# Layer 2's residual loads: issued with the transposes, or two images ahead behind the sums

## The chip, the cores and the metric

The kernel runs on one core of a Trainium2 chip. The metric is the time of one execution on the device in microseconds (us); the kernel before takes 3451.94 us, the median of 3 runs (3447.39 to 3453.05). The engines are named as the profile names them: PE multiplies matrices, DVE and ACT and POOL compute on vectors, SP only issues transfers (DMA).

## The reference

The input is 8 images of 384 channels and 32 x 32 pixels, in float32. Four layers follow one another; each adds its result to its input, and each normalizes its input over groups of 12 channels first:

```python
x = x + L0(_gn(x))   # depthwise 3x3, GELU, attention over the 1024 pixels, projection, batch norm
x = x + L1(_gn(x))   # 4 experts of 384 hidden units, top 2 by a gate
x = x + L2(_gn(x), w, b)   # depthwise 7x7
x = x + L3(_gn(x))   # 1x1, 3x3 and 5x5 branches, mixed by weights from their means, projection

def L2(x, w, b):
    xp = pad(x, 3, mode="reflect")
    return depthwise_conv(xp, w) + b[None, :, None, None]
```

The change is in the layer called 2 here (counted from 0): the depthwise 7x7 convolution, its bias, and the addition of its input, which is called the residual.

## The kernel before

**Tiles.** The 384 channels are three channel tiles `ct` of 128, which is the number of partitions. When layer 1 has finished an image, it writes the image to memory outside the core (`r2mem[ct]`, lines 998 to 1003), where it waits as the residual, and puts the normalized image transposed into `xts[ct]`, for tile 2 by way of `x2mem`.

**The convolution** (lines 1281 to 1324). For each tile there are 8 chunks `c`. A chunk is 7 rows of taps times 16 products of 32 x 32 matrices over all 8 images, thus 112 matmuls; a float32 matmul stands as two records in the trace, so 224 records. Two chunks fill one of the two PSUM tiles, which ACT copies out into `o` (`evict`, line 1236). Each chunk has a set of weights of 532 KB. `next_weights` (line 1035) issues the load of the set three chunks ahead on SP, line 1046, and adds the reflected edges to it on POOL, line 1052. There are three weight buffers (`lw`, line 1027), so a set can be loaded when PE is through with the set three before it.

**Finishing an image.** When tile `ct` has been convolved, `finish_all(ct, o)` (line 1181) finishes its 8 images while PE convolves the next tile. For each image, `finish` (line 1152) is a generator of two steps:

- step one takes an `r2` tile and loads the residual into it (line 1154, 512 KB, on SP), and turns the image back by a transpose on DVE (line 1157);
- step two is the sum of the convolved image, the bias and the residual on DVE (line 1159), the store of the sum to `y2mem` (line 1162, 512 KB, on SP), and statistics: `bn_stats`, and for tiles 0 and 1 sums of the rows and columns at the edge (lines 1170 and 1174 on DVE, 1176 on POOL).

For tiles 0 and 1 `lead` is 8: all first steps come before the first sum. For tile 2 `lead` is 2: the first step of image b + 2 comes ahead of the sum of image b. The pool `ty` (line 1083) has two `r2` buffers, so the load for image b + 2 can start only when the sum of image b has read its buffer. Between the sums of tile 0, `prepare` (line 1138) loads tile 2's images from `x2mem` (line 1143, tile `xn2`) and DVE transposes them (line 985). Late in tile 2's convolution, `prepare3` (line 1202) loads the finished sums again, as halves of images (line 1214), for the convolutions of layer 3.

**What sets the order.** From line 1279 on, PE, ACT, DVE and POOL run their instructions in the order in which the program writes them:

```python
with tc.manual_schedule(engines=ORDERED | {mybir.EngineType.Pool}):
```

SP is not among them. Its instructions are put in order by the framework's scheduler, when it expects each to be ready. The order is fixed when the program is built. SP then works through it one by one: an instruction that waits, for a buffer or for data, holds up all behind it. So the weight loads, the residual loads, the stores and the loads of `x2mem` all stand in one line.

## Time and profile before

| | |
|---|---|
| median of 3 runs | 3451.94 us (3447.39 to 3453.05) |
| the profiled execution | 3453.2 us, of which the span that the profile shows is 3451.5 us |
| busy in the span | PE 3085.5 us (89%), DVE 1610.4 (47%), ACT 1202.3 (35%), POOL 140.8 (4%) |
| the 7x7 convolution with tile 0, nothing to finish (2882 to 2962 us) | PE busy 58.2 of 80.0 us, granted clock 0.89 |
| mostly tile 1, tile 0's images finished (2962 to 3047 us) | PE busy 46.4 of 85.0 us, granted clock 0.84 |
| mostly tile 2, tile 1's images finished (3047 to 3098 us) | PE busy 32.7 of 51.0 us, granted clock 0.80 |
| after it, 3x3 and 5x5 begin, tile 2's images finished (3098 to 3192 us) | PE busy 51.0 of 94.0 us, granted clock 0.57 |

Times within the execution are counted from the start of the span. A line of the timeline gives the start, the busy time, the engine (SPq is SP's queue of issues), the line of the program, the operation, what is written and read, the shape and the number of instructions; in brackets stand the idle time before it and what ended that. The granted clock is the share of full speed that PE got. The wait of a DMA instruction on SP is not busy time; it is seen in the view of waits.

### The profile page before, as it was taken

What the parts mean: (1) busy time and instruction counts of PE and PEld (TensorE: products, weight loads), DVE (VectorE), ACT (ScalarE), POOL (GpSimd) and SP (SyncE); (2) the same over time, 40 slices, a digit from 0 to 9 for tenths busy, and PEclk for the clock granted to TensorE, in tenths of its full rate; (3) what the DMA queues carried; (4) which work ended last, traced back from release to release, by engine and by line L of the source; (5) the groups of instructions that cost most, each with busy time, mean ns of one, the idle gap of its engine ahead of it and who ended that gap; (6) DMA issues with size and microseconds to landing.
All of it is one profiled execution on the core that took longest, in us unless ns stands there. A gap on an engine that the chain in (4) does not pass through costs nothing. (4 is left out here: it accounts for less than half of the span.)

```text
span 3451.5 us, 56137 instructions
## 1 busy us (share of the span) xinstructions
PE 3085.5 (89%) x24960; PEld 1403.8 (41%) x24960; DVE 1610.4 (47%) x2193; ACT 1202.3 (35%) x1147; POOL 140.8 (4%) x320
## 2 busy tenths in 40 slices
PE   3666999999999999999979999999999997555889
PEld 2443334343434343433333444444444444334434
DVE  6778344444454544444442654333333321546164
ACT  3654453535454444445324302122222211123320
POOL 1000000000000000000000000000000000110200
PEclk9998999999999999999989999999999998885989
DMA  6766202011111010110017222022111103556655
GB/s 223 250 235 229 99 21 76 21 60 36 57 39 57 30 61 27 55 42 19 23 49 270 85 90 86 28 67 76 32 63 64 41 8 117 194 171 199 224 198 200
DMA packets 97251, 338.49 MB, mean 98 GB/s; under 512 B 13985, under 2 KB 16777, under 8 KB 92457
## 3 DMA queue, kind: packets, MB, share of 16 engines
q1 hardware_dynamic: 81816, 285.81, 23.9%
q0 software_dynamic: 9184, 32.49, 2.7%
q10 hardware_dynamic: 6000, 16.53, 1.6%
q8 instruction: 197, 3.23, 0.4%
q14 instruction: 54, 0.43, 0.0%
HBM read 236.39 MB, written 101.53 MB: 98 GB/s over the span
## 5 line engine op out<-in xcount | busy, mean ns | idle before, releaser
L548 ACT ACTIVATE e<-sc 128x1024 f32<-128x1024 f32 x512 | 484.2, 1029 | 583.0 <-PE sc L541 582.6
L759 PE MATMUL ph<-xn,w 128*128 128x512 f32 x1152 | 525.0, 594 | 1.2 <-ACT xn L200 1.2
L972 PE MATMUL y<-hs,w 128*128 128x512 f32 x1152 | 519.9, 593 | 1.5 <-DVE hs L957 1.5
L541 PE MATMUL sc<-qT,kT 64*128 64x512 f32 x2048 | 481.7, 607 | 22.1 <-DVE qT L467 15.4
L560 PE MATMUL av<-e,vT 128*64 128x512 f32 x2048 | 468.9, 600 | 0.0
L763 ACT ACTIVATE hs<-ph,b 128x512 f32<-128x512 f32 x192 | 131.7, 686 | 630.9 <-PE ph L759 629.3
L972 PEld LDWEIGHTS y<-hs,w 128*128 128x128 f32 x1152 | 217.8, 190 | 274.4 <-issue 263.5
L759 PEld LDWEIGHTS ph<-xn,w 128*128 128x128 f32 x1152 | 216.3, 190 | 268.3 <-issue 258.8
L541 PEld LDWEIGHTS sc<-qT,kT 64*128 64x128 f32 x2048 | 186.5, 186 | 309.9 <-issue 232.0
L957 DVE TENSOR_TENSOR hs<-hs,cb 128x512 f32<-128x512 f32 x192 | 130.7, 690 | 355.6 <-ACT hs L763 348.6
L560 PEld LDWEIGHTS av<-e,vT 128*64 128x64 f32 x2048 | 135.9, 137 | 318.6 <-issue 318.6
L449 PE MATMUL sc<-y,pw 128*128 128x512 f32 x576 | 254.1, 602 | 12.0 <-DVE kT L467 7.3
L325 PE MATMUL ps<-xt,w 32*32 32x256 f32 x6912 | 161.9, 418 | 106.8 <-issue 106.8
L576 DVE RECIPROCAL inv<-sm 128x512 f32<-128x512 f32 x64 | 214.6, 3353 | 2.2
L1291 PE MATMUL ps<-xt,w 32*32 32x256 f32 x5376 | 135.2, 438 | 82.4 <-POOL w L1052 39.6
L574 DVE LOAD_MASK_SELECT sm<-av x64 | 0.9, 14 | 417.1 <-PE av L560 417.1
L962 DVE SCALAR_TENSOR_TENSOR r<-cb,b,r 128x512 f32<-128x512 f32 x192 | 134.9, 744 | 91.0 <-DMA cb<-cfmem 89.4
L325 PEld LDWEIGHTS ps<-xt,w 32*32 32x32 f32 x6912 | 109.8, 107 | 158.5 <-issue 136.3
L449 PEld LDWEIGHTS sc<-y,pw 128*128 128x128 f32 x576 | 110.4, 193 | 155.2 <-issue 147.2
L350 ACT COPY o<-ps 128x2048 f32<-128x2048 f32 x36 | 134.6, 3739 | 102.0 <-PE ps L325 101.3
L1291 PEld LDWEIGHTS ps<-xt,w 32*32 32x32 f32 x5376 | 91.9, 110 | 124.5 <-issue 56.9
L1236 ACT COPY o<-ps 128x2048 f32<-128x2048 f32 x20 | 73.9, 3694 | 173.2 <-PE ps L1291 151.6
(285 smaller groups left out, 2680.8 us busy)
## 6 DMA issues: line engine op xcount, KB each, us to landing
raw<-y SPq DMA_DIRECT2D x72, 512.0 KB
y<-raw SPq DMA_DIRECT2D x24, 1536.0 KB
xr<-in_x SPq DMA_DIRECT2D x42, 512.0 KB
cb<-cfmem SPq DMA_DIRECT2D x64, 256.0 KB
w<-in_w ACTq DMA_DIRECT2D x36, 384.0 KB
w<-in_w SPq DMA_DIRECT2D x24, 532.0 KB
x<-in_x SPq DMA_DIRECT2D x16, 768.0 KB
z<-z POOLq DMA_DIRECT2D x16, 768.0 KB, 4.3
```

Source lines behind the costliest of these rows:

```text
L325: nc.tensor.matmul(ps[32 * j : 32 * j + 32, i, cc], lhsT=w[r, cc, j, k, :], rhs=xt0s[ct][r, 8 * j + 2 * u + cc, :, k : k + H], start=k == ...
L350: nc.scalar.copy(o.rearrange("p b h (i c) -> p i c (b h)", i=4)[:, :, 2 * u : 2 * u + 2], ps.rearrange("p i c b h -> p i c (b h)"),)
L449: nc.tensor.matmul(ps[:, h, :], lhsT=w[:, ct, pair, :], rhs=y[:, ct, h * HF : (h + 1) * HF], start=ct == 0, stop=ct == NC - 1,)
L541: nc.tensor.matmul(sc[:, s, :], lhsT=kTs[b][r, pair, m * P : (m + 1) * P], rhs=qTs[b][r, pair, h * HF : (h + 1) * HF], start=True, stop=True,)
L548: nc.scalar.activation(e, sc, AF.Exp, scale=1.0 if shifted else HD**-0.5)
L560: nc.tensor.matmul(av[64 * s : 64 * s + 64, :], lhsT=vT[:, m, c0 : c0 + 64], rhs=e[:, s, :], start=m == 0, stop=m == N // P - 1,)
L576: nc.vector.reciprocal(inv, sm)
L759: nc.tensor.matmul(ph, lhsT=w1[:, e, ct, dc * P : (dc + 1) * P], rhs=xn[:, ct, :], start=ct == 0, stop=ct == NC - 1,)
L763: nc.scalar.activation(hs, ph, AF.Relu, bias=b1[:, e, dc : dc + 1])
L962: nc.vector.scalar_tensor_tensor(out=out[oc], in0=cb[e], scalar=b2[:, oc, e : e + 1], in1=out[oc], op0=ALU.mult, op1=ALU.add,)
L972: nc.tensor.matmul(py[oc], lhsT=w2[:, e, dc, oc * P : (oc + 1) * P], rhs=hs, start=k == 0, stop=k == len(TODO) - 1,)
L1291: nc.tensor.matmul(ps[32 * j : 32 * j + 32, i, c % 2], lhsT=w[r, j, k, :W], rhs=xts[ct][r, 8 * j + c, :, k : k + H], start=k == 0, stop=k ...
```

## The change

The residual's load leaves the first step and becomes a step of its own, between the transpose and the sum. `finish_all` runs that step for images 0 and 1 when `lead` images have been transposed (at `b == lead - 1`), and afterwards for image b + 2 behind the sum of image b.

```diff
     def finish(ct, b, o, y):
-        r2 = ty.tile([P, N], FP, tag="r2", name="r2")
-        nc.sync.dma_start(out=r2, in_=r2mem[ct][:, b, :])
         if y is None:
             y = new_y()
         nc.vector.transpose(img(y), o[:, b])
+        yield
+        r2 = ty.tile([P, N], FP, tag="r2", name="r2")
+        nc.sync.dma_start(out=r2, in_=r2mem[ct][:, b, :])
         yield
         nc.vector.scalar_tensor_tensor(
             out=y, in0=y, scalar=b7[:, ct : ct + 1], in1=r2, op0=ALU.add, op1=ALU.add
...
         for b in range(B + lead):
             if b < B:
                 next(steps[b])
+            if b == lead - 1:
+                next(steps[0])
+                next(steps[1])
             if b >= lead:
                 next(steps[b - lead], None)
+                if b - lead + 2 < B:
+                    next(steps[b - lead + 2])
             if b >= lead - 1:
                 yield
```

The number of transfers, their sizes and the two buffers stay as they are. In the changed program the residual's load stands in line 1158, the sum in line 1160 and the store in line 1163.

## The prediction

> **What bounds the kernel now.** I read the slices first: TensorE (PE) is busy in 9 tenths of nearly the whole span and falls to 5 to 7 tenths only at the start and from about 2870 us on, where layer 2 stands. The listing of PE's instructions by line names the loss there: L1291, the 7x7 convolution, waits for POOL's L1052, the folding of freshly loaded weights. The timeline of PE gives each such wait (start, busy us, then in brackets the idle time before it and who ended it):

> ```profile
> 2966.78 4.65 PE L1291 MATMUL ps<-xt,w 32*32 32x256 f32 x145 [3.52 <-POOL w L1052]
> ...
> 2983.56 5.61 PE L1291 MATMUL ps<-xt,w 32*32 32x256 f32 x176 [8.82 <-POOL w L1052]
> ...
> 2993.40 4.57 PE L1291 MATMUL ps<-xt,w 32*32 32x256 f32 x208 [1.32 <-POOL w L1052]
> ...
> 3011.12 9.47 PE L1291 MATMUL ps<-xt,w 32*32 32x256 f32 x367 [10.21 <-POOL w L1052]
> ...
> 3047.45 0.65 PE L1291 MATMUL ps<-xt,w 32*32 32x256 f32 x12 [2.70 <-POOL w L1052]
> ...
> 3063.90 6.15 PE L1291 MATMUL ps<-xt,w 32*32 32x256 f32 x172 [9.26 <-POOL w L1052]
> ...
> 3075.87 6.30 PE L1291 MATMUL ps<-xt,w 32*32 32x256 f32 x224 [3.73 <-POOL w L1052]
> ```

> They sum to 39.6 us, 1.1% of the span. A chunk is 224 records, so counting records tells which chunk starts after each: chunks 3, 4, 5, 6 of channel tile 1 (stage A, while tile 0's images are finished) and 3, 4, 5 of tile 2 (stage B, while tile 1's are). I call their weight loads W3 to W6 and W3' to W5', the sum of image b S0 to S7 (S0' to S7' in B), its residual load r0 to r7 and its store y0 to y7. POOL folds each set as soon as it has landed, so the loads are late, and SP issues them all, in order. The waits of SP's queue from 2944 to 3070 us (line, releaser, us, times, longest):

> ```profile
> SPq L1154 <- DVE x L1159: 37.0, 8, 13.7
> SPq L1046 <- PE ps L1291: 22.3, 3, 11.8
> SPq L1154 <- DVE y L1159: 14.3, 4, 8.4
> ```

> So SP stands 51.3 us at residual loads whose two buffers are held until a sum is done, with weight loads behind it. That looks like 39.6 us to win. What decides is what SP meets instead.

> **What the change does to the queues.** Built both ways, PE, ACT, DVE and POOL run the same instructions in the same order; only SP's order differs. In A it was: r2 y0 **W3** xn r3 y1 xn xn xn r4 **W4** y2 xn r5 y3 xn **W5** r6 y4 r7 y5 y6 r0' y7 r1' **W6**; it becomes y0 r2 **W3** xn y1 r3 xn xn xn y2 **W4** r4 xn y3 r5 xn **W5** y4 r6 y5 r7 y6 r0' y7 r1' **W6**. Before, r(b+2) waited for S(b) to free a buffer, and y(b) stood behind it. Now y(b) waits for the same S(b), and r(b+2) stands behind it. SP is blocked at the same instants by the same sums. In B one load moves: W4' stood behind r7', which waits for S5', and now stands behind y4', which waits for S4'.

> ```profile
> 2957.93 0.33 SPq L1154 DMA_DIRECT2D r<-r  x1
> 2958.30 1.11 SPq L1162 DMA_DIRECT2D y<-x  x1
> 2959.52 0.38 SPq L1046 DMA_DIRECT2D w<-in_w  x1
> ...
> 3056.76 0.32 SPq L1154 DMA_DIRECT2D r<-r  x1
> 3057.18 0.38 SPq L1046 DMA_DIRECT2D w<-in_w  x1
> ...
> 3065.64 0.52 SPq L1046 DMA_DIRECT2D w<-in_w  x1
> ```

> This is SP's timeline: r2 goes at 2957.93, the end of S0, then y0, then W3. With y0 first, W3 still goes at 2959.5.

> **Term 1, W3, W4, W5, W3': 0.** Each stays two issues or fewer behind the same sum (S0, S2, S3, S0'), behind as many transfers of the same size.

> **Term 2, residuals one transfer later in A.** r(b+2) now travels behind y(b). From the trace's records of landings: r6 landed at 2997.27 and y4, behind it, at 2998.60; r7 at 3001.07 and y5 at 3002.37. One place costs 1.3 us. S2 to S5 have their residuals 3 us or more ahead and hide it. S6 started at 2998.19 and would start at 2998.6; S7 at 3001.37 becomes 3002.4. y7, which waits for S7, goes 1.0 later, and W6 with it. The chain of waits shows W6, which took 6.60 us to land:

> ```profile
> 3003.56 6.60 DMA w<-in_w
> ...
> 3042.01 6.39 DMA r<-r
> 3049.74 5.69 DMA r<-r
> ...
> 3068.16 11.47 DMA w<-in_w
> ```

> With 6.60 again, chunk 6 starts 1.0 later. If the queue, not the issue, sets the landing (y7 3.6 us after its issue, then two places of 1.3) it starts no later than now. I take **+0.9**, nearest the row, bounds 0 and +1.1. All of B shifts by it.

> **Term 3, the same in B.** Here the sums already wait for residuals, as the timeline of DVE shows, so the cover is gone:

> ```profile
> 3048.42 1.28 DVE L1159 SCALAR_TENSOR_TENSOR x<-x,b,r 128x1024 f32<-128x1024 f32 x1 [1.25 <-DMA r<-r]
> ...
> 3055.45 1.28 DVE L1159 SCALAR_TENSOR_TENSOR y<-y,b,r 128x1024 f32<-128x1024 f32 x1 [0.57 <-DMA r<-r]
> ...
> 3154.80 1.28 DVE L1159 SCALAR_TENSOR_TENSOR y<-y,b,r 128x1024 f32<-128x1024 f32 x1 [1.80 <-DMA r<-r]
> ```

> r2' would land at 3044.5 instead of 3042.8 and start S2' 0.6 late; r3', behind y1', at 3049.8 instead of 3048.4; S4' runs at 3053.0 instead of 3051.6 and ends at 3054.3.

> **Term 4, W4'.** It goes behind y4' at 3054.8 instead of 3057.2. It landed 5.8 us after its issue, at 3062.95; that again gives 3060.5, and places of 1.3 us behind the four transfers still under way 3059.4. Taking 3060.0, chunk 4 starts at 3061.0 instead of 3063.9: 2.9 earlier.

> **Term 5, W5'.** A gain at chunk 4 counts only as far as chunk 5 follows. r6' is now behind W4' and lands near 3061.2, so S6' (3058.6) starts 2.6 late, and y7' goes at 3065.7 instead of 3063.1. W5' stands behind y7' and two half-image loads, at 3067.2 instead of 3065.6. Before, eight places took it from W4''s 3062.95 to 3074.91, 1.5 us each; now nine from 3060.0 give 3073.5. So chunk 5 starts **1.4 us earlier** than its 3075.87, bounds 3.5 earlier (places of 1.3) and 1.5 later (W5' keeping its 9.3 us from the issue). Everything after it (norm, 5x5 and 3x3, projection) shifts with chunk 5: W6' stays hidden, landing before chunk 5 ends.

> **Term 6, stage C (tile 2's images, 3112 to 3158): 0.** S7'' would end 1.3 later, at 3158.7 with its statistics; the norm that needs it starts on PE at 3171.6, 13 us later. Without that cover it would cost the 1.3.

> **The clock.** The busy time by stretch, with the clock granted, shows what the clock does to a chunk: chunk 4 of B took 8.24 us at 0.66, chunk 6 of B 6.58 at 1.00. That is the bound for an unlucky wait: plus or minus 2.

> [...]

> **Sum.** 0 + 0.9 - 1.4 + 0 = **-0.5 us**. The profiled execution took 3453.2 us (span 3451.5), 1.3 above the median 3451.94; it becomes 3452.7, and the median **3451.4**. A measurement of this kernel tells about 0.2% (6.9 us) from no change: its three runs already differ by 5.7. Own bounds: 0 - 3.5 - 2 to 1.1 + 1.5 + 2, so -5.5 to +4.6.

> **Rival 1, slower: residuals become DVE's pace.** From the end of S(b) to the start of S(b+2) lie 5.1 us (two periods of 3.2 less a sum of 1.28). In B r3' took 6.39 and r5' 5.69 from issue to landing. If the store ahead makes it 7.7 in steady state, two sums cost 7.7 + 1.28 = 9.0 instead of 6.4, or 1.3 per sum: S2' to S7' lose 7.8, of which 1.8 is already paid, 6 net. y7' and W5' go 6 later, A adds 1.0 and the clock up to 2: +7 to +9, **3460**. It decides from a residual latency of about 7.4 us. For it: the waits above. Against it: stores and residuals alternate at DVE's pace, and DVE's own lateness drains the queue. Chance 0.14.

> **Rival 2, faster: the weights come free.** If the 51.3 us of SP's blocking were the residuals' own, W4 to W6 would start chunks on time and up to 39.6 us would go. Against: SP's order shows each but W4' at the same sum. W3' to W5' alone (15.7) reach 10 if chunk 5 keeps all that W4' wins and its own wait goes: **3442**. Chance 0.13.

> **Rival 3, nothing moves at all:** stores and loads change places and each wait takes the other's: 3451.9, inside the forecast's range.

> **How the numbers follow.** Forecast with rival 3: 0.73. Range 3443.5 to 3458.5: the own bounds (3446.4 to 3456.5), opened toward both rivals. Faster by over 0.2% 0.13, within 0.73, slower 0.14.

> **What would show it.** SP's waits move from L1154 to the y store (L1163), about 45 to 50 us in total. W3 to W5 leave PE's waits 3.5, 8.8, 1.3 as they are; chunk 6's becomes about 11; chunk 4's in B falls to about 6.4 and chunk 5's rises to about 5. DVE waits for residuals at S6, S7, S2', S3', S6'. I am wrong if chunk 4 in A loses its 8.8, or if DVE waits over 1 us at most of S2' to S7'.

## The result, and the profile after

The changed kernel takes 3446.98 us, the median of 20 runs (3436.36 to 3453.71); the kernel before took 3451.23 in 20 runs on the same chip (3443.49 to 3458.95). The ratio is 0.9988, with a 95% interval from 0.998 to 0.9996: 4.2 us, or 0.12%, less. That is within the 0.2% of no change, inside the predicted range and 4.4 us below the predicted 3451.4. The profiled execution took 3449.4 us, with a span of 3447.6.

The seven waits of PE for a folded set of weights are still there. This is PE's timeline of the kernel after, as it was shown of the kernel before (start, busy us, then in brackets the idle time and who ended it):

```profile
2963.98 4.65 PE L1297 MATMUL ps<-xt,w 32*32 32x256 f32 x145 [3.29 <-POOL w L1052]
...
2980.27 5.75 PE L1297 MATMUL ps<-xt,w 32*32 32x256 f32 x176 [6.56 <-POOL w L1052]
...
2989.66 4.57 PE L1297 MATMUL ps<-xt,w 32*32 32x256 f32 x208 [0.56 <-POOL w L1052]
...
3008.04 9.21 PE L1297 MATMUL ps<-xt,w 32*32 32x256 f32 x367 [12.04 <-POOL w L1052]
...
3043.41 4.43 PE L1297 MATMUL ps<-xt,w 32*32 32x256 f32 x140 [3.64 <-POOL w L1052]
...
3058.38 6.70 PE L1297 MATMUL ps<-xt,w 32*32 32x256 f32 x224 [7.50 <-POOL w L1052]
...
3073.66 6.35 PE L1297 MATMUL ps<-xt,w 32*32 32x256 f32 x224 [8.57 <-POOL w L1052]
```

They are chunks 3, 4, 5 and 6 of stage A and 3, 4 and 5 of stage B, and sum to 42.2 us, against 39.6 before. Chunk 4 waits less in both stages (8.82 to 6.56, 9.26 to 7.50); chunk 6 of A (10.21 to 12.04) and chunk 5 of B (3.73 to 8.57) wait more.

The waits of SP's queue from 2944 to 3070 us have moved from the residual's load to the store:

```profile
SPq L1163 <- DVE x L1160: 41.2, 8, 13.7
SPq L1163 <- DVE y L1160: 25.5, 8, 7.8
SPq L1046 <- PE ps L1297: 18.3, 2, 12.7
```

SP stands 66.7 us at stores. Before it stood 51.3 us at residual loads for the sums, and the same view of the kernel before has two more lines, for stores and for residual loads that wait for an earlier one:

```profile
SPq L1162 <- DVE y L1159: 8.8, 4, 2.8
...
SPq L1154 <- DMA r<-r: 4.6, 3, 2.4
```

That is 64.7 us in all. SP is blocked by the same sums for about as long; the change renamed the wait.

The sums on DVE now wait for residuals at four places (S7, S2', S3', S6') instead of two in stages A and B:

```profile
2997.80 1.28 DVE L1160 SCALAR_TENSOR_TENSOR y<-y,b,r 128x1024 f32<-128x1024 f32 x1 [0.40 <-DMA r<-r]
...
3041.20 1.28 DVE L1160 SCALAR_TENSOR_TENSOR x<-x,b,r 128x1024 f32<-128x1024 f32 x1 [1.38 <-DMA r<-r]
...
3045.20 1.29 DVE L1160 SCALAR_TENSOR_TENSOR x<-x,b,r 128x1024 f32<-128x1024 f32 x1 [0.71 <-DMA r<-r]
...
3058.74 1.28 DVE L1160 SCALAR_TENSOR_TENSOR y<-y,b,r 128x1024 f32<-128x1024 f32 x1 [3.83 <-DMA r<-r]
```

The largest one has its cause in SP's timeline. W4' goes at 3050.12, early as intended; r6', one place behind it, goes at 3050.58, and the chain of waits gives it 8.13 us to land. S6' waits for it, y7' waits for S7' (3063.24), and W5' stands behind y7' (3065.04):

```profile
3050.12 0.37 SPq L1046 DMA_DIRECT2D w<-in_w  x1
3050.58 0.71 SPq L1158 DMA_DIRECT2D r<-r  x1
...
3063.24 0.33 SPq L1163 DMA_DIRECT2D y<-y  x1
...
3065.04 0.53 SPq L1046 DMA_DIRECT2D w<-in_w  x1
```

```profile
3038.22 6.95 DMA r<-r
...
3050.58 8.13 DMA r<-r
...
3068.23 9.18 DMA w<-in_w
```

**Where the two traces differ.** Three stages can be cut at the same events in every kernel: A from S0 to S0', B from S0' to the first weight load of the 5x5 on PE, C from there to that of the gate's matmul. A went from 80.9 to 78.8 us, B from 73.1 to 74.6, C from 77.7 to 75.8; S0 came 2.0 us earlier, ahead of any instruction that the change moves, and what follows C took 0.8 longer. I predicted +0.9 for A and, from S0' to chunk 5 of B, -1.4; the two profiles show -2.1 and +1.9 there. So the total is near the forecast, and its parts are not: this is what the experiments are for.

### The profile page after: what moved, and what is told of

Read it like the earlier page. It is cut to its first block, busy times and chain, and to the rows that moved or that the text cites. A ratio compares the mean times of both kernels' runs of the same rounds, so it can differ in the third digit from the quotient of the medians.

```text
span 3447.6 us, 56141 instructions
## 1 busy us (share of the span) xinstructions
PE 3091.5 (90%) x24960; PEld 1408.8 (41%) x24960; DVE 1610.2 (47%) x2193; ACT 1202.2 (35%) x1147; POOL 139.9 (4%) x320
## 5 line engine op out<-in xcount | busy, mean ns | idle before, releaser
L541 PE MATMUL sc<-qT,kT 64*128 64x512 f32 x2048 | 482.0, 607 | 22.2 <-DVE qT L467 15.4
L325 PE MATMUL ps<-xt,w 32*32 32x256 f32 x6912 | 170.2, 441 | 98.5 <-issue 98.5
L1297 PE MATMUL ps<-xt,w 32*32 32x256 f32 x5376 | 134.4, 436 | 81.8 <-POOL w L1052 42.2
```

The costliest lines, as they stand in the source:

```text
L325: nc.tensor.matmul(ps[32 * j : 32 * j + 32, i, cc], lhsT=w[r, cc, j, k, :], rhs=xt0s[ct][r, 8 * j + 2 * u + cc, :, k : k + H], start=k == ...
L541: nc.tensor.matmul(sc[:, s, :], lhsT=kTs[b][r, pair, m * P : (m + 1) * P], rhs=qTs[b][r, pair, h * HF : (h + 1) * HF], start=True, stop=True,)
L1297: nc.tensor.matmul(ps[32 * j : 32 * j + 32, i, c % 2], lhsT=w[r, j, k, :W], rhs=xts[ct][r, 8 * j + c, :, k : k + H], start=k == 0, stop=k ...
```

## The experiments

The theories at the start: (T1) a store at the head of SP's pair lands sooner than a load does, and this gives A its 2 us; (T2) in B the early W4' pushes r6' back, and chunk 5 gives back what chunk 4 won; against both, (N) the differences between single executions are chance. Later a third came up: (T3) PE has pauses of its own, and time won at the weights is lost there. Every run is compared with the kernel before on the same chip; its median there was 3441.4 for the first four, 3443.7 for the next four, 3450.2 for the three after and 3452.9 for the last.

| run | median us | ratio to before (95%) | A | B | C |
|---|---|---|---|---|---|
| kernel before (profiled) | 3451.2 | 1 | 80.9 | 73.1 | 77.7 |
| kernel after | 3447.0 | 0.9988 (0.998 to 0.9996) | 78.8 | 74.6 | 75.8 |
| 1: change in A alone | 3444.1 | 1.0002 (0.9992 to 1.0012) | 81.6 | 73.4 | 77.1 |
| 2: change in B alone | 3441.2 | 0.9996 (0.9985 to 1.0007) | 80.9 | 72.0 | 72.7 |
| 3: change in C alone | 3444.4 | 1.0000 (0.9986 to 1.0014) | 81.2 | 74.3 | 72.8 |
| 4: load ahead of the store | 3444.4 | 1.0000 (0.9991 to 1.0009) | 80.4 | 71.8 | 76.5 |
| 5: before, sets on ACT's queue | 3434.0 | 0.9962 (0.9947 to 0.9977) | 76.6 | 68.2 | 73.9 |
| 6: after, sets on ACT's queue | 3429.0 | 0.9956 (0.994 to 0.9973) | 75.3 | 68.6 | 71.9 |
| 7: after, residuals and stores on ACT's queue | 3433.8 | 0.9972 (0.9961 to 0.9984) | 70.1 | 68.7 | 78.8 |
| 8: after, again | 3443.8 | 0.9997 (0.9984 to 1.001) | 79.6 | 73.3 | 74.6 |
| 9: a quarter of each residual | 3436.4 | 0.9952 (0.9935 to 0.9969) | 75.9 | 66.9 | 71.9 |
| 10: after, sets on POOL's queue | 3434.8 | 0.9947 (0.9929 to 0.9966) | 66.8 | 72.3 | 75.0 |
| 11: extra loads in tile 0's stage | 3461.6 | 1.0027 (1.0007 to 1.0048) | 79.6 | 72.2 | 78.0 |
| 12: before, sets on POOL's queue | 3437.8 | 0.9952 (0.9939 to 0.9965) | 66.3 | 71.5 | 75.2 |

### Runs 1 to 3: the change in one stage at a time

With `late = ct in (0,)`, `(1,)` or `(2,)`:

```diff
     def finish(ct, b, o, y):
+        late = ct in (0,)
+        if not late:
+            r2 = ty.tile([P, N], FP, tag="r2", name="r2")
+            nc.sync.dma_start(out=r2, in_=r2mem[ct][:, b, :])
...
-            if b == lead - 1:
+            late = ct in (0,)
+            if b == lead - 1 and late:
...
-                if b - lead + 2 < B:
+                if b - lead + 2 < B and late:
```

Run 1, A alone:

> The change for tile 0's images alone: in stage A the store goes ahead of the residual's load, in B and C the order is the old one. Stage A is measured from the first transpose of tile 0's images on DVE to the first of tile 1's: 80.9 us before, 78.8 us after. Theory 1 (a store at the head of SP's pair lands about 1 us sooner than a load does, so the pair and the x2mem and weight loads behind it land 1 to 1.8 us sooner, and chunk 4's wait on PE falls from 8.8 to about 6.6): A 78.8 within 0.7, W3 landing 5.5 us after its issue (6.3 before), the pairs 4.7 to 5.8 us (5.5 to 6.6 before). Rival (A's 2.1 us are chance, like the 2.0 us that the two traces differ by ahead of the first changed instruction): A anywhere between 78 and 82, with chunk 4's wait near 8.8. My recorded term 2: A 81.8. B, unchanged here but for y7, keeps its old 47.4 us up to chunk 5 by both. Time: 3449 by theory 1, 3451 by the rival.

Run 2, B alone:

> The change for tile 1's images alone: A and C have the old order; in B the set W4' goes behind y4' instead of behind r7'. Stage B is measured from the first transpose of tile 1's images to the start of chunk 5 of tile 2: 47.4 us before, 49.3 us after. Theory 2 (chunk 4 gains by the earlier W4', but r6' behind it takes 8 us to land, S6' waits 3 to 4 us, y7' and W5' come late and chunk 5 gives it all back): B 49.3 within 0.7, chunk 5's wait 8 us or more, S6' waiting 3 us or more. Rival (the 1.9 us are chance, or come from A's earlier end): B 46 to 47.4, as my recorded terms 3 to 5 have it (chunk 5 1.4 us earlier), chunk 5's wait near 5. A as before, near 80.9, with chunk 4's wait 8.8. Time: 3453 by theory 2, 3450.5 by the rival.

Run 3, C alone:

> The change for tile 2's images alone; A and B have the old order. Stage C is measured from the first matmul of the 5x5 to that of the gate (hbias): 77.6 us before, 75.6 us after; A and B serve as a second look at the old order. If the change in C makes the difference: 75.6 within 0.5. If it is the clock and the gaps between issues on PE, which no part of the change touches (my recorded term 6, 0): 76 to 78, with DVE's one wait for a residual of 1.8 us gone or not without an effect on PE. A near 80.9 and B near 47.4 with chunk 4's wait in A near 8.8 if the stages follow the program; A or B 2 us off those if the stages scatter by themselves. Time: 3450 if C counts, 3452 if not.

None of the three differs from the kernel before in time. In the stages they give, with runs 4 and 8, a second to fourth profile of each order. The starts of the chunks that matter, counted from S0 (A) or S0' (B), in us:

| kernel | order in A | A: chunk 4 | A: chunk 6 | order in B | B: chunk 4 | B: chunk 5 |
|---|---|---|---|---|---|---|
| before | old | 26.9 | 54.5 | old | 26.3 | 38.3 |
| run 3 | old | 28.8 | 54.7 | old | 26.9 | 37.7 |
| run 2 | old | 28.7 | 55.3 | new | 22.9 | 37.6 |
| run 1 | new | 26.4 | 55.4 | old | 26.2 | 37.6 |
| after | new | 25.6 | 53.4 | new | 25.0 | 40.3 |
| run 8 | new | 25.7 | 54.3 | new | 23.7 | 38.7 |
| run 4 | old | 28.6 | 55.3 | W4' early, behind r6' | 24.7 | 39.1 |

In A, chunk 4 starts 2.4 us earlier with the new order (25.9 in the mean of three, 28.2 in the mean of four), without overlap. Its set W4 shows why: S2, which SP waits for ahead of it, starts 16.0 to 17.3 us after S0 with the new order and 17.6 to 18.3 with the old, and W4 lands 24.5 to 25.4 us after S0 against 25.9 to 27.8. So the first half of theory 1 holds: with the store at the head, what stands behind it lands sooner. Two rows of PE's timeline of run 1 (new order in A) show what becomes of it:

```profile
2972.64 6.11 PE L1303 MATMUL ps<-xt,w 32*32 32x256 f32 x176 [8.38 <-POOL w L1052]
...
3001.64 9.21 PE L1303 MATMUL ps<-xt,w 32*32 32x256 f32 x367 [12.56 <-POOL w L1052]
```

and the same rows of run 3 (old order in A):

```profile
2978.87 5.25 PE L1303 MATMUL ps<-xt,w 32*32 32x256 f32 x176 [10.70 <-POOL w L1052]
...
3004.84 9.48 PE L1303 MATMUL ps<-xt,w 32*32 32x256 f32 x367 [9.71 <-POOL w L1052]
```

Chunk 4 waits 2.3 us less, and chunk 6 waits 2.9 us more. W6 stands behind y7, which waits for S7, and in run 1 the sums S4 to S7 start 3.1 to 3.7 us apart on DVE. By chunk 6 the two orders are 0.6 us apart (54.4 against 55.0), with a scatter of 2 within the new order, and the stage is 80.0 in the mean against 80.9. So of A's 2.1 us about 1 may belong to the change, though the two ranges overlap (78.8 to 81.6 against 80.4 to 81.2), and the rest is chance.

In B, chunk 4 gains with W4' early (23.9 in the mean of three, against 26.5) and chunk 5 gives it back (38.8 against 37.9). Run 2 was to show B, from its transposes to chunk 5, at 49.3 by theory 2; it was 46.6, with S6' waiting 1.7 us and not 3. The order does what theory 2 says (chunk 5 waits 7.97, with W4' early), but chunk 5 comes between 0.3 us before and 2.4 us after the old order's mean. The 1.9 us that B lost between the first two traces were near the high end.

C took 72.8 us with the change and 72.7 without it (run 2). In five profiles with the old or the new order there it lay between 74.6 and 77.7. The change does nothing in C that one profile can show.

### Run 4: the load ahead of the store

```diff
             out=y, in0=y, scalar=b7[:, ct : ct + 1], in1=r2, op0=ALU.add, op1=ALU.add
         )
+        yield
         nc.sync.dma_start(out=y2mem[b][ct], in_=y)
...
                 if b - lead + 2 < B:
                     next(steps[b - lead + 2])
+                next(steps[b - lead], None)
```

> The changed kernel, but within a step the residual's load is issued ahead of the store, as before the change. In A and C SP's order is then the old one; in B W4' stands behind r6' and ahead of y4', so that it is early as in the changed kernel but r6' is not behind it. Theory 1 (the store at the head is what A gains by): A back to 80.9 within 0.7, chunk 4's wait 8.8, W3 landing after 6.3. Rival (A scatters): no such return need be seen. Theory 2 (in B it is r6' behind W4' that takes the gain back): S6' waits less than 1.5 us instead of 3.8, y7' and W5' are issued 2 to 3 us sooner after chunk 4's start than in the changed kernel, and B is 45.5 to 47 instead of 49.3. Rival to theory 2 (the memory queue is full, the order within it does not count): B 48.5 to 49.5, chunk 5's wait 8 again. Time: 3449 to 3452.

A's chunk 4 went back to 28.6, among the old ones, so what brings it forward is the place of the store. The length of A went back to 80.4 only, and W3 landed 5.7 us after its issue, not 6.3. For theory 2 the run is a miss on both sides: S6' waited 1.8 us (under 1.5 expected), y7' was issued 27.7 us after S0' (25.6 to 25.9 in the old order, 27.8 to 29.8 in the new), and B up to chunk 5 took 48.2. Putting r6' ahead of W4' doesn't mend B. In both orders with W4' early S6' starts late (22.5 us after S0' here, 23.3 to 25.3 in the new order, 20.5 to 21.1 in the old). That this is the 532 KB of W4' among the residuals, whatever its place, fits, but is not shown by this run alone.

### Runs 5 and 6: the sets of weights on ACT's queue

```diff
-        nc.sync.dma_start(out=w, in_=a["w7" if n == K7 else f"w3{n}"][unit, c])
+        nc.scalar.dma_start(out=w, in_=a["w7" if n == K7 else f"w3{n}"][unit, c])
```

Run 5, on the kernel before:

> The kernel before, but next_weights issues its loads on ACT's queue instead of SP's; the residuals keep their old order. It asks whether the order on SP is what makes the sets late at all. Theory (head-of-line blocking: a set waits on SP behind a load or store that waits for a sum): the sets are issued as soon as PE is through with the set three before, land 3.5 to 7 us later, and PE's waits for POOL w fall from 39.6 us to under 10; the time falls by 10 to 30 us, to 3412 to 3432 on a chip that gives 3441 before, less than the 30 us where the sums, the x2mem loads and the transposes on DVE become what PE waits for. Rival (the memory traffic, not the issue, sets the landings: some 200 GB/s in these stages): the waits stay above 30 us and the time within 5 us of before.

Run 6, on the changed kernel:

> The changed kernel with the weight loads on ACT's queue. With the weights off SP the change has nothing left to give or take there, except what the residuals cost DVE. If my terms 2 and 3 are right in kind (a residual behind a store makes sums late, by 1 to 2 us in all of A and in B), this is 0 to 4 us slower than the same move made on the kernel before; if the store at the head of the pair helps (it landed about 1 us sooner than a load at the head in four runs so far), it is 0 to 3 us faster. Against the kernel before: 10 to 30 us faster by head-of-line blocking, within 5 us by the rival of memory traffic.

Both are faster than before, by 9.7 and 14.7 us in their medians; their intervals overlap, so they don't tell the two orders of residuals apart. The waits for sets fell to 15.7 and 18.0 us, not under 10. In run 6 one of the two that are left is seen on ACT's timeline. Its issues stand from 2964.72 on, and the copy behind them is released by a residual's landing:

```profile
2964.72 24.87 ACTq L1046 DMA_DIRECT2D w<-in_w  x2
2989.63 3.66 ACT L1242 COPY o<-ps 128x2048 f32<-128x2048 f32 x1 [28.70 <-DMA r<-r]
```

By the landing records, r6 landed at 2989.16 and the set was issued at 2989.26; both signal the same counter (118). In the traces of the kernels before and after, the transfers of SP's and ACT's queues signal the same eight counters and POOL's eight others. That the set waited for the residual is my reading of the 0.10 us between them. The other late set was issued at 3049.37, 0.15 us after a store of SP's queue landed on counter 100; the text below on run 10 calls both of them residual loads.

What was not expected is that 24 us less of waiting brought 15 us at most. The lines of PE in the listing by line (busy us, mean ns, then the idle time and what ended it) say where it went. Before:

```profile
L1291 PE MATMUL ps<-xt,w 32*32 32x256 f32 x5376 | 135.2, 438 | 82.4 <-POOL w L1052 39.6 <-issue 37.6 <-POOL xt L988 5.1
```

Run 5:

```profile
L1291 PE MATMUL ps<-xt,w 32*32 32x256 f32 x5376 | 136.0, 443 | 74.2 <-issue 53.3 <-POOL w L1052 15.7 <-POOL xt L988 5.1
```

The waits for sets fell by 23.9 us, and the idle time called issue, in which PE waits for nothing that the profile names, rose by 15.7 (37.6 to 53.3).

### Run 7: residuals and stores on ACT's queue

```diff
-        nc.sync.dma_start(out=r2, in_=r2mem[ct][:, b, :])
+        nc.scalar.dma_start(out=r2, in_=r2mem[ct][:, b, :])
...
-        nc.sync.dma_start(out=y2mem[b][ct], in_=y)
+        nc.scalar.dma_start(out=y2mem[b][ct], in_=y)
```

> The changed kernel with the residual loads and the stores of the sums on ACT's queue, and the weights left on SP. The weights then wait on SP only for the x2mem loads; ACT, which copies PSUM out, can be held by a store that waits for a sum. Head-of-line blocking: W3 to W6 early, PE's waits for POOL w below 15 us, but new waits of PE for ACT's copies where ACT stands at a store, up to the same size; time 10 to 25 us below before, or level where ACT's copies come late by as much. Rival of memory traffic: within 5 us of before, PE's waits for w above 30.

PE's waits for sets fell to 6.2 us and A to 70.1, as head-of-line blocking has it. PE never waited for one of ACT's copies, which had been expected; instead DVE waited 22.8 us for residuals in A and B (6.3 in the kernel after), once for 10.6 us. The time fell by 9.9 us only: issue rose to 55.1 us, and C was the longest of all, 78.8.

### Run 8: the changed kernel again

> The changed kernel once more, on this chip, to see how much of the first comparison's 4.2 us (ratio 0.9988, interval 0.998 to 0.9996) comes again, and how far one execution of the same kernel scatters in each stage. If the change is worth 4 us: ratio 0.9980 to 0.9995 again. If the change is worth nothing and the first figure was near the edge of chance, as the three runs with one stage changed suggest (1.0002, 0.9996, 1.0000): 0.9990 to 1.0010. In the profile: from S0 to S0' 78.8 us came once with the change and 81.6 once; a third value near 79 would speak for a gain in A, 80.5 to 81.5 for none.

The ratio is 0.9997, and 1 is inside its interval. A came out at 79.6 us, between its two earlier values. The first comparison gave 0.9988, with an interval that leaves 1 out and ends at 0.2%. So the two measurements of the change put it 1 and 4 us below before, and the three runs with one stage changed lie between 1.4 us below and 0.7 above; none of these intervals reaches beyond 0.2%.

### Run 9: a quarter of each residual

```diff
-        nc.sync.dma_start(out=r2, in_=r2mem[ct][:, b, :])
+        nc.sync.dma_start(out=r2[:, : N // 4], in_=r2mem[ct][:, b, : N // 4])
...
-            out=y, in0=y, scalar=b7[:, ct : ct + 1], in1=r2, op0=ALU.add, op1=ALU.add
+            out=y.rearrange("p (a n) -> p a n", a=4), in0=y.rearrange("p (a n) -> p a n", a=4),
+            scalar=b7[:, ct : ct + 1],
+            in1=r2[:, None, : N // 4].to_broadcast([P, 4, N // 4]), op0=ALU.add, op1=ALU.add
```

> The changed kernel with a quarter of each residual's bytes: 128 x 256 instead of 128 x 1024 are loaded, and the sum reads that quarter four times, so the output lacks three quarters of the residual. SP's order keeps its kind (W4 and W4' stand one place later). It bounds what any order of the residual loads can win. If the lateness of the residuals and their bytes hold chunk 5 of B (r6' behind W4', S6' late, y7' late, W5' late): no wait of DVE for a residual, y7' issued about 25.6 us after S0' starts as in the old order or sooner (27.7 to 29.8 in the runs with W4' early), W5' landed 33 to 35 us after S0' (36.6 to 39.3 in all runs so far), and the time 4 to 10 us below before. Rival (what PE does not wait for at the weights it pauses for by itself: the pauses that the profile calls issue, after every 127 or 128 records, 0.7 to 1.2 us each where transfers are few and up to 5 us where they crowd): the weights land sooner, but the pauses grow by half or more of it, and the time is within 4 us of before.

The first theory holds in kind, and both of its sizes were too small. DVE waits for a residual once (0.81 us), y7' is issued 24.4 us after S0', W5' lands 31.8 us after it (33 to 35 expected), chunk 5 of B waits 0.85 us instead of 8.57, and the time falls by 13.7 us (4 to 10 expected). The pauses called issue stay at 34.4 us (34.5 in the kernel after). So in B it is the residuals' bytes and their lateness that hold chunk 5; this run doesn't separate the two. The waits for sets do not go away, though: they still sum to 32.9 us, with 9.78 at chunk 4 of A and 9.27 at chunk 4 of B. No order of full residuals removes their bytes, so the 13.7 us are a rough bound for what reordering the residuals could win.

### Runs 10 and 12: the 7x7 sets on POOL's queue

```diff
-        nc.sync.dma_start(out=w, in_=a["w7" if n == K7 else f"w3{n}"][unit, c])
+        queue = nc.gpsimd if n == K7 else nc.sync
+        queue.dma_start(out=w, in_=a["w7" if n == K7 else f"w3{n}"][unit, c])
```

Run 10, on the changed kernel:

> The changed kernel with the 7x7 sets loaded by POOL's queue, ahead of the fold of the same set. With the loads on ACT two waits for sets were left (11.4 and 6.7 us), each a set that ACT issued late, at the instant a residual load of SP's landed. Theory (those were waits of ACT for a counter that the two queues share, no shortage of transfers): on POOL's own queue all sets are issued when PE is through with the set three before, and PE's waits for sets fall below 5 us from 42; the pauses called issue grow with it, from 31 to 50 us or more, so that the time falls by 12 to 25 us only. Rival (the sets are late because the transfers are slow): waits for sets stay above 15 us and the time is 5 to 15 us below before, as with ACT's queue.

Run 12, on the kernel before:

> The kernel before, without the change, with the 7x7 sets on POOL's queue: the pair to the run that did the same to the changed kernel (ratio 0.9947, PE's waits for sets 0, pauses called issue 63.0 us, DVE waiting 9.3 us for residuals in A and B). It asks what the order of the residuals is worth when no weight stands behind it. If the residual's load behind the store costs (my recorded terms 2 and 3): DVE waits under 4 us for residuals, S0' to the 5x5 is 68 to 71 us instead of 72.3, ratio 0.9930 to 0.9940. If the order is worth nothing in either direction because the pauses of PE and not the sums set the pace: waits for sets 0, pauses 58 to 66 us, A within 2 us of 66.8, ratio 0.9940 to 0.9955.

PE's line in run 10:

```profile
L1298 PE MATMUL ps<-xt,w 32*32 32x256 f32 x5376 | 132.9, 433 | 68.3 <-issue 63.0 <-POOL xt L988 5.1
```

and in run 12:

```profile
L1292 PE MATMUL ps<-xt,w 32*32 32x256 f32 x5376 | 133.7, 439 | 65.8 <-issue 60.6 <-POOL xt L988 5.1
```

Against the line of the kernel after:

```profile
L1297 PE MATMUL ps<-xt,w 32*32 32x256 f32 x5376 | 134.4, 436 | 81.8 <-POOL w L1052 42.2 <-issue 34.5 <-POOL xt L988 5.1
```

No wait for a set is left, of 42.2 us; issue rose by 28.5, and PE's idle time in the convolution fell by 13.5 (81.8 to 68.3). The times are 15.3 and 15.1 us below before, the ratios 0.9947 and 0.9952 with intervals that overlap. With no weight behind the residuals DVE waits for them 8.3 us in A and B in the new order (the text for run 12 has 9.3) and 4.9 in the old, and no difference in time can be told: this is run 12's second theory. These two are the best versions of this study that compute the whole reference, together with run 6.

### Run 11: extra loads where nothing else travels

```diff
                 if c % 2:
                     evict(o, ps, c - 1)
+                    if ct == 0 and c < 7:
+                        for i in range(6):
+                            d = ty.tile([P, N], FP, tag="r2", name="r2")
+                            nc.scalar.dma_start(out=d, in_=r2mem[0][:, i, :])
```

> The changed kernel with 18 loads of 512 KB that nothing reads, six behind each of the first three PSUM copies of tile 0's convolution, on ACT's queue, in the stage in which only weights travel otherwise. It asks whether the pauses of PE called issue depend on what else travels. In the 80 us window of that stage (20 us ahead of the first 7x7 matmul's long wait to 2945) they sum to 16.7 to 17.2 us in 12 to 14 pauses in four runs. Theory (in a pause PE waits for something that comes by the same transfers, its own instructions most likely): the pauses that fall into the extra loads grow to 2 to 5 us each, the sum to 25 us or more, and the stage from the first 7x7 matmul to S0 becomes 6 to 15 us longer; the time 6 to 15 us above before. Rival (PE pauses by its own count alone): sum 16 to 18 us, the time within 3 us of before.

From the first 7x7 matmul to S0 the kernel took 82.8 us, against 73.0 in the kernel after, and the whole 9 us (by the ratio) to 11 us (by the medians) more than before. From 2881 to 2962 us PE paused 11 times for 2.0 us each in the mean, 22.2 us in all (kernel after: 18 times, 1.1, 20.3 in all); the 25 us expected were not reached, because PE often ran 255 records instead of 128 between pauses. Tile 0's convolution by itself took 69.9 us instead of 60.2. Of the difference the pauses are 4.4 us (10 of them, 20.7 us, against 13 and 16.3), and 5.4 are busy time (49.3 against 43.9), at a mean granted clock of 0.79 instead of 0.91. So the theory holds for the single pause (2.0 us against 1.1), but the larger part of the lost time is slower work and not waiting. PE's timeline of the kernel after in the quiet part of this stage:

```profile
2923.97 2.79 PE L1297 MATMUL ps<-xt,w 32*32 32x256 f32 x128 [1.22 <-issue]
2927.71 2.86 PE L1297 MATMUL ps<-xt,w 32*32 32x256 f32 x128 [0.96 <-issue]
2931.83 2.78 PE L1297 MATMUL ps<-xt,w 32*32 32x256 f32 x127 [1.26 <-issue]
2935.22 2.78 PE L1297 MATMUL ps<-xt,w 32*32 32x256 f32 x128 [0.61 <-issue]
```

and in run 11:

```profile
2927.02 6.69 PE L1297 MATMUL ps<-xt,w 32*32 32x256 f32 x255 [3.43 <-issue]
2936.96 6.71 PE L1297 MATMUL ps<-xt,w 32*32 32x256 f32 x255 [3.25 <-issue]
2946.51 4.07 PE L1297 MATMUL ps<-xt,w 32*32 32x256 f32 x128 [2.84 <-issue]
```

A lower clock (0.79 against 0.91) came with the longer pauses; that they are its cause was not tested apart. The busy time by stretch (the last three columns are the granted clock, the DMA share and GB/s) is, in the kernel after,

```profile
2930.00:2945.00 15.00, 10.96 (x510) 7.29 (x491) 0.00 (x0) 5.33 (x2) 1.49 (x4) 1.00 0.32 108
```

and in run 11

```profile
2930.00:2945.00 15.00, 10.43 (x436) 8.16 (x410) 0.00 (x0) 3.75 (x1) 0.81 (x3) 0.88 0.70 232
```

**What the pauses are.** The page of the kernel after lists the DMA queues (packets, MB, share of the 16 engines):

```profile
q8 instruction: 197, 3.23, 0.4%
```

A packet of this queue has 16,384 bytes in the trace. From 2882 to 3100 us, PE resumes after a pause called issue within 1.1 to 1.7 us of the end of such a packet in 31 of 32 cases in the kernel after, 31 of 32 before, 35 of 37 in run 10 and 24 of 25 in run 11. With 42 such packets in these 218 us in the kernels before and after, I estimate that chance would put about one case in nine there. The 5376 records of the convolution, each a matmul with a weight load beside it, come to 128 for each of the 42 packets, and between two pauses PE mostly runs 127 or 128 of them, or 255 or 256. My reading is that in these pauses PE waits for its own instructions, one packet for so many records; no run changed the packets alone. A long wait for a set seems to cover such a pause: behind the 12.04 us of chunk 6, PE runs 367 records without one. This is T3, and by it 42.2 us of waiting were worth 13.5 us of idle time in run 10, where issue rose by 28.5. Covered pauses are the smaller part of it: in tiles 1 and 2 the kernel after pauses 18 times for 1.0 us in the mean, run 10 24 times for 1.9. Whether the pauses grow because PE is sooner through with its code or because more transfers travel beside it was not separated. Run 9, with a quarter of each residual's bytes, lost 9.3 us of waits for sets, and its pauses did not grow (34.4 us against 34.5). In run 11, with more transfers under way (a DMA share of 0.70 instead of 0.32 from 2930 to 2945 us), they were longer.

## Why the prediction was right, and which steps were not

**The forecast** (no change that can be measured, 0.73) came about, and the mechanism that carried it held: SP is blocked by the same sums, under another line's name. That the sum of the terms came close as well is partly luck: A came 0.9 us shorter in the mean instead of 0.9 longer, chunk 5 of B 1.0 later instead of 1.4 earlier, and the two errors cancel.

**Term 1 (W3, W4, W5, W3': 0)** failed for W4. I counted places in the queue and took them as equal. With the store in front, chunk 4 of A came 2.4 us earlier (three profiles against four, and run 4 took it back). The sign that I was wrong (chunk 4 in A loses its 8.8) came in part: its wait was 6.56, 8.38 and 9.01 us in the three profiles with the new order.

**Term 2 (+0.9 in A)** did not come; in the mean the sign was the other. S7 waits 0.2 to 0.4 us for r7 instead of the 1.0 I gave it (and 0.4 once in the old order); S6 doesn't wait. Chunk 6 comes 0.6 us earlier in the mean, within the scatter; that this is what term 1's gain leaves is not shown.

**Term 3 (S2', S3' and S4' up to 1.4 late)** held. S4' starts 14.8 to 15.1 us after S0' in the three profiles with the new order and 13.4 to 14.1 in the three with the old: 1.4 later in the mean.

**Term 4 (chunk 4 of B 2.9 earlier)** held: 2.6 earlier, in three profiles against three.

**Term 5 (chunk 5 of B 1.4 earlier)** is the step that failed. The places were right and the delay too small. From W4' to W5' I gave nine places of 1.5 us, 13.5 in all; the runs show 15.0 (landed 22.9 and 37.9 us after S0' in the mean), and W4' itself landed 0.5 later than I had it. S6' comes 3.3 us later in the mean (24.2 us after S0' against 20.9) and not 2.6, because r6' lands one place of 1.3 behind the later W4'. W5' is issued 30.2 to 31.6 us after S0' where I had 29.6: the issues between y7' and W5' took 2.3 us in the mean, and I had 1.5. So chunk 5 came 1.0 later in the mean, inside the bound of 1.5 that I gave it, and all of term 4 is lost.

**Term 6 (C: 0)** stands: 72.8 with the change, 72.7 without.

**The clock.** The two chunks that I took the bound of 2 us from are not alike: the 6.58 us of chunk 6 hold 1.7 us of idle time, and chunk 5, at a clock of 0.68, took 6.23, so they do not show what the clock does to a chunk. In the kernel after chunk 5 took 6.35 us at a granted clock of 0.74 behind a wait of 8.57; before it took 6.30 at 0.69 behind 3.73. The longer wait cost it no speed there, and whether a wait of PE brings a lower clock was not tested.

**The rivals.** Rival 1 needed a residual latency of 7.4 us in steady state. In B it was 6.14, 6.95, 5.03, 4.68, 8.13 and 7.86 us: it passes the mark only next to W4'. Two of the six sums S2' to S7' wait over 1 us, not most. Rival 2 did not come: the waits for sets sum to 42.2 us. Run 10 did remove them all, and the 39.6 us which I took as their price were not to be had: 14 us of idle time went.

**What I said would show it.** The waits did move to L1163, but to 66.7 us and not 45 to 50: I had left out the 8.8 us that the stores already waited, and the rest of the difference I cannot account for. DVE waited for residuals where I said, but for S6. Chunk 6 rose to 12.0 (about 11 said), chunk 4 of B fell to 7.5 (6.4) and chunk 5 rose to 8.6 (5).

**Where the 4.2 us came from** stays partly open. About 1 us in A may have a mechanism (the store at the head); 2.0 us arose ahead of the first moved instruction; C's 2.0 lie within a scatter of 5 us between executions of the same order; run 8 found 0.9997.

## What to carry to other kernels

Ask, before moving a transfer in an in-order queue, which event the queue stands at: if the neighbour that takes its place waits for the same event, only the name of the wait may change, as here (64.7 us of SP's waits became 66.7). Price a wait by what the engine would meet next: in run 10 PE's pauses called issue grew by 28.5 us when its 42.2 us of waits for weights went, and its idle time fell by 13.5. What helped was another queue for the transfers that must not wait (9.7 to 15.3 us), not another order in the same one.
